# A block with a linear scan and an FP4 feed-forward part: VectorE's order within a slot, later modulation products, a partition maximum through DRAM, and three down products in a row at the end

## The chip, the cores and the metric

The kernel runs on one core of a Trainium2 chip. The time is the device time of one execution in microseconds (us); lower is better. Five engines work side by side, each through its own queue of instructions in order: TensorE (PE; PEld are its weight loads), VectorE (DVE), ScalarE (ACT), GpSimd (POOL) and SyncE (SP), which here only issues DMAs. GpSimd issues some DMAs too. Engines wait for each other through semaphores.

## What is computed

Two batches of 4096 tokens, 512 wide, pass through one block: an adaptive norm, a gated linear recurrence as attention, a second adaptive norm, and a feed-forward part of inner width 1408 whose inputs and weights are rounded to FP4 in blocks of 16 values with one scale each.

```python
mod = (silu(c) @ wmod).reshape(2, 6, 1, -1)
sa, ca, ga, sb, cb, gb = (mod[:, j] for j in range(6))     # ga, gb: |.| floored at 0.25, sign kept
h = layernorm(x) * (1 + ca) + sa
xn = h / norm(h) * sqrt(512) * gamma
q, kv, a = split(xn @ W_qkva.T, 3)
y_t = sigmoid(a_t) * y_{t-1} + kv_t                        # along the tokens
x = x + ga * (q * y)
h = layernorm(x) * (1 + cb) + sb
gate, up = fp4(h) @ fp4(w_gate).T, fp4(h) @ fp4(w_up).T
x = x + gb * (fp4(silu(gate) * up) @ fp4(w_down).T)
```

## The kernel before

Every matrix product runs in three passes over 16-bit halves (high x high, high x low, low x high), so an operand lies in memory as a high and a low part side by side, `hl`, which a transposing DMA on SP turns round.

**The first part** is a loop over slots. There are 16 blocks of 512 tokens (`NBLK`) with 4 feature chunks each (`KC`), so 64 slots with products and 3 more to drain. Slot s issues `mix` s on PE: 36 products of 512 columns, three results (a, kv, q) in three of six PSUM banks, so that mix s + 1 can be in work while mix s is evicted and mix s + 2 cannot. In the same slot the results of mix s - 1 are evicted: `gates` (sigmoid on ACT, L401), `scan` (VectorE, L407, with a small ACT copy `cy` of the last column, L410), `read_out` (VectorE, L416), `halves` (ACT copy L423, transposing DMA of `yt` on SP), and two slots later `joined` (ACT copy L431) and `residual` (GpSimd addition L439 and its DMA to the output, L441). Beside it the slot prepares tokens: `norm_hi` (ACT, L363) and `norm_lo` (VectorE, L368, followed by the transposing DMA of `xT` on SP) for the tile 4 ahead, statistics of the tile 6 ahead (L151, L156, then two small GpSimd steps L158 and L159), `norm_center`, `norm_shift`, `norm_square` and `norm_gain` (L164, L170, L350, L355 and L357) of the tile 5 ahead. The first mix of a block, every fourth slot, needs the block's whole `xT`.

The slots also carry the FP4 weights as units. `plan` gives them to slots: first maxima of blocks (`weight_max`, two units a slot, executed in slots 6 to 22), then `finish_max` (slot 23), which takes the maximum over the partitions with a GpSimd instruction, then one quantizing unit a slot (`quant_rows`, `quant_down`, 34 of them). A unit's weight tile is loaded one slot ahead by SP. `quant` is a chain in seven steps: reciprocal and `sh` (L101, L103); `xn`, `sl`, `she` (L107, L109, L113); absolute value and `sle` on ACT (L116, L118); rounding in two VectorE steps (L120, L123); two products (L125, L127); then a transposing DMA. `Unit.advance(n)` takes one step; the positions of these calls in the loop set where the steps stand in each engine's queue, since the whole order is written out by hand (`manual_schedule`).

The modulation vectors: `mod` 1 and 0 are computed in `start`, 2 in slot 0, and 3, 4 and 5 in slots 1, 2 and 3 (`mod_rows`, L229). `mod_store`, one slot later, copies the two rows by ACT into `row`, whose buffer has the tag of `sig`, and GpSimd sends it to DRAM (`modd`, L259). Each takes 1 MB of weights by `load_mod`. In slots 0 to 2, `hi_qkva` and `lo_qkva` also prepare the weights of the next mix (`wqT`).

**The second part** loops over 64 tiles of 128 tokens. Iteration i issues on PE `products(i)` (72 products, L827) and `down(i - 2)` (33 products, L877), with two PSUM banks for the latter; VectorE, ACT and SP gate, quantize and transpose in between, and `finish` (L897, L900) evicts a down product and adds it to the output by DMA. The last down product is made in two halves of 256 columns.

Of the kernel before, what the change touches and what calls it, by code (L numbers as in the profile page):

```python
# [44 lines left out]
def tile_adaln_block(  # L45
# [51 lines left out]

    def quant(src, sb, rt, nb, hl):

        inv = small.tile([P, nb], F32, name="inv", tag=f"inv{nb}", bufs=2)  # L100
        V.reciprocal(inv, sb)  # L101
        sh = small.tile([P, nb], BF16, name="sh", tag=f"sh{nb}", bufs=2)
        A.activation(sh, sb, AF.Copy, scale=rt)  # L103
        yield
        pool, w = (ring, INTER) if nb == NBH else (work, D)
        xn = pool.tile([P, w], F32, name="xn", tag=f"xn{w}", bufs=1)[:, : nb * QB]
        V.tensor_tensor(blocks(xn), blocks(src), spread(inv, nb), ALU.mult)  # L107
        sl = small.tile([P, nb], F32, name="sl", tag=f"sl{nb}", bufs=2)
        V.scalar_tensor_tensor(  # L109
            out=sl, in0=sb, scalar=rt, in1=sh, op0=ALU.mult, op1=ALU.subtract  # L110
        )
        she = pool.tile([P, w], BF16, name="she", tag=f"she{w}", bufs=1)[:, : nb * QB]
        A.activation(blocks(she), spread(sh, nb), AF.Copy, scale=WPEAK)  # L113
        yield
        a = src
        A.activation(a, xn, AF.Abs, scale=MAGIC)  # L116
        sle = pool.tile([P, w], F16, name="sle", tag=f"sle{w}", bufs=1)[:, : nb * QB]
        A.activation(blocks(sle), spread(sl, nb), AF.Copy, scale=WPEAK)  # L118
        yield
        V.scalar_tensor_tensor(out=xn, in0=a, scalar=FLOOR, in1=xn, op0=ALU.max, op1=ALU.add)  # L120
        yield
        nq = hl[:, 0, :]
        V.scalar_tensor_tensor(out=nq, in0=a, scalar=FLOOR, in1=xn, op0=ALU.max, op1=ALU.subtract)  # L123
        yield
        V.tensor_tensor(hl[:, 1, :], nq, sle, ALU.mult)  # L125
        yield
        V.tensor_tensor(nq, nq, she, ALU.mult)  # L127
# [47 lines left out]
    def load_tile():  # L175
        return work.tile([P, D], F32, name="ld", tag="ld", bufs=7)

# [75 lines left out]
    def mod_store(s, pm):  # L253
        row = apool.tile([B, D], F32, name="row", tag="sig", bufs=1)
        if s == 5:
            signed_floor(row, pm, apool.tile([B, D], F32, name="mag", tag="y", bufs=3))
        else:
            A.activation(row, pm, AF.Copy, bias=1.0 if s in (1, 4) else 0.0)
        G.dma_start(modd[s], row)  # L259
# [203 lines left out]
    def weight_max(wt, am, col, first):  # L463
# [4 lines left out]
        else:  # L468
            m = small.tile([P, 1], F32, name="gm", tag="gm")
            V.tensor_reduce(m, am, AX.X, ALU.max)  # L470
            V.tensor_tensor(gsum[:, col : col + 1], gsum[:, col : col + 1], m, ALU.max)

    def finish_max():
        gs = small.tile([P, 3], F32, name="gs", tag="gs", bufs=1)
        G.partition_all_reduce(gs, gsum, P, bass_isa.ReduceOp.max)
# [12 lines left out]
    def quant_rows(wt, i, am, col):  # L488
        dst = weights(("wgT", "wuT")[col], col, [P, 2 * KC, INTER])
        hl = new_hl()  # L490
        yield from quant(wt, am, rwk[:, col : col + 1], NBX, hl)
        S.dma_start_transpose(dst[:, :, i * P : (i + 1) * P], flat(hl))
# [8 lines left out]
    def quant_down(wt, i, j):  # L501
# [4 lines left out]
        yield from quant(  # L506
            wt, am_d[i][j], rwk[:, 2:3], w // QB, hl.rearrange("p (a d) -> p a d", a=2)
        )
# [10 lines left out]
    for n in range(0, len(downs), 2):  # L519
        plan.append([("maxd", r) for r in downs[n : n + 2]])  # L520
    plan.append([("finish", None)])
    for n, r in enumerate(rows):
# [68 lines left out]
    class Unit:  # L591
# [9 lines left out]
        def advance(self, pos):  # L601
# [4 lines left out]
            elif pos == 3:  # L606
                if self.kind == "max":
                    i, col, _, ams = self.arg
                    weight_max(self.wt, ams[i], col, i == 0)
                elif self.kind == "maxd":  # L610
                    i, j = self.arg
                    weight_max(self.wt, am_d[i][j], 2, self.arg == (0, 0))
                else:
                    finish_max()
# [5 lines left out]
    def start():  # L620
        load_mod(1, 2)
        norm_load(0)
        load_part(0, 2)
        S.dma_start(gam, gamma.partition_broadcast(P))
# [3 lines left out]
        load_part(0, 1)  # L628
        load_mod(0, 2)
        load_part(1, 2)  # L630
# [92 lines left out]
    joining = []  # L723
    NS = NBLK * KC
    plan = [[]] * (KC + 1) + plan
    order = tc.manual_schedule(engines={V.engine, A.engine, G.engine, S.engine, T.engine})
    with order:
        xT = new_xT()
        start()
        for slot in range(NS + 3):  # L730
            i, e = divmod(slot, KC)
            if e == 0 and slot < NS:
                if slot:
                    xT = nxT
                nxT = new_xT() if i + 1 < NBLK else None
            units = [u for u in units + [Unit(*c_) for c_ in coming] if u.step < 7]
            coming = load_units(plan[slot]) if slot < len(plan) else []
            g = slot + KC
# [5 lines left out]
            if slot == 0:  # L744
                cols = mod_columns(2)
            elif slot < KC:
                rows = mod_rows(2 + slot)
            if 0 < slot < 3:
# [3 lines left out]
            if gate is not None:  # L752
                gate = gates(*gate)
            for u in units:
                u.advance(0)
            if len(joining) == 2 or slot >= NS + 2:
# [9 lines left out]
            if slot == 1:  # L766
                signed_floor(gq, cols, atile([P, KC, B], F32, "mag"))
                prep_gain(0)
            if gate is not None:
                joining.append(halves(*read_out(*gate)))  # L770
            if g + 2 < NT:
                norm_moments(g + 2)
                norm_stats(g + 2)
            for u in units:
                u.advance(1)
            if g < NT:
                norm_lo(g, nxT)
            for u in units:
                u.advance(2)
            if g + 1 < NT:  # L780
                norm_center(g + 1)
                norm_shift(g + 1)
                norm_square(g + 1)
                norm_gain(g + 1, G)
            for n in range(3, 7):
                for u in units:
                    u.advance(n)
            if slot < 2:
                scale_qkva(slot + 2)
            if 0 < slot < KC:  # L790
                prep_gain(slot)
            if i == 0 and e < 3:
                load_mod(3 + e)
            if late is not None:
# [14 lines left out]
    tc.no_sync_barrier()  # L809
    assert all(u.step == 7 for u in units)  # L810
    wgT, wuT, wdT = wts["wgT"], wts["wuT"], wts["wdT"]
# [56 lines left out]
    def down(i):  # L868
        hT, u = qh.pop(i)
        width = D // 2 if i == NT - 1 else D  # L870
        pds = []
        for d in range(0, D, width):
            pd = side((P, width))
            n = 0
            for k in range(IC):
                for hp, wp in PASSES:
                    T.matmul(  # L877
                        pd,
                        hT[:, hp * IC + k, :],
                        wdT[:, wd_chunk(wp, k), d : d + width],  # L880
                        start=n == 0,
                        stop=n == 3 * IC - 1,
                    )
                    n += 1
            pds.append(pd)
        return i, pds, u

    def finish(i, pds, u):
        b, t0 = divmod(i * P, N)
# [4 lines left out]
        o = ring.tile([P, D], F32, name="o", tag="o", bufs=3)  # L894
        for n, pd in enumerate(pds):
            d = slice(n * D // len(pds), (n + 1) * D // len(pds))
            V.scalar_tensor_tensor(  # L897
                out=o[:, d], in0=pd, scalar=u, in1=gbs[b][:, d], op0=ALU.mult, op1=ALU.mult
            )
# [10 lines left out]


    with tc.manual_schedule(engines={V.engine, A.engine, G.engine, S.engine, T.engine}):
        h = None
        ended = None
        for i in range(NT + LAG):
            work_i = products(i) if i < NT else None
            ending, ended = ended, down(i - LAG) if i >= LAG else None
            x = None
# [7 lines left out]
            step(h, 2)  # L926
            if work_i is not None:
                sl = silu(0, *work_i)
# [4 lines left out]
            if work_i is not None:  # L933
                gated(0, sl, *work_i)
            step(x)
            if work_i is not None:
                sl = silu(1, *work_i)
            step(x)
            if ending is not None:
                finish(*ending)  # L940
            step(x, 4)
            if work_i is not None:
                gated(1, sl, *work_i)
                gated(2, silu(2, *work_i), *work_i)
                h = quant_h(i, work_i[2])
                step(h, 3)
            else:
                h = None
        finish(*ended)


# [39 lines left out]
```

## Time and profile before

| what | us |
|---|---|
| time, median of 3 runs (1988.0 to 1989.73) | 1988.95 |
| the profiled execution | 1986.11 |
| its span in the profile | 1984.3 |
| PE busy in it | 1920.1 |
| DVE busy | 1622.3 |
| ACT busy | 993.3 |
| POOL busy | 435.2 |
| mean granted PE clock | 0.986 |

A row of the profile's group list shows the source line, the engine and the operation, what is written from what, a count, then busy time and the mean of one in ns, and at the end how long the engine stood idle ahead of it and what ended that. A row of the timeline shows start and length in us and, in brackets, the idle time before it and its releaser. Products on PE are pipelined, and their ends are modelled. A small count of them has no record.

### The profile page before, as it was taken

The numbers are of one execution on the slowest core, as the hardware profiler recorded it, in microseconds if no ns is written. First come the engines' busy times: TensorE is split into PE (matmuls) and PEld (weight loads), VectorE is DVE, ScalarE is ACT, GpSimd is POOL, SyncE is SP. The second block draws the span as 40 slices with busy tenths as digits, with TensorE's granted clock in tenths as the row PEclk, the third lists the DMA queues.
The fourth block names the chain that finished last, engine by engine and source line by source line (L and its number), as shares of the span: only waits on it lengthen the run. The fifth ranks groups of instructions, "written<-read, shape, count | busy, mean of one in ns | idle before, by whom it ended". The sixth has DMA issues, their size and how long they took to land.

```text
span 1984.3 us, 25684 instructions
## 1 busy us (share of the span) xinstructions
PE 1920.1 (97%) x9253; PEld 907.7 (46%) x9253; DVE 1622.3 (82%) x2672; ACT 993.3 (50%) x1704; POOL 435.2 (22%) x602
## 2 busy tenths in 40 slices
PE   7799989999999999999999999999999999999997
PEld 4244434444444444444444444444444444444444
DVE  5679879999966998888888888888888888888874
ACT  3355557777764554444454454455454454444431
POOL 3455546656631110000001001001000000000000
PEclk8999999999999999999999999999999999999998
DMA  7677758888852434334334334434433433433423
GB/s 228 160 180 205 189 143 190 190 185 188 184 134 70 80 69 84 70 62 81 72 61 78 75 62 87 78 62 81 78 62 72 81 62 68 82 64 65 78 46 51
DMA packets 482847, 206.19 MB, mean 104 GB/s; under 512 B 439446, under 2 KB 440726, under 8 KB 482720
## 3 DMA queue, kind: packets, MB, share of 16 engines
q1 hardware_dynamic: 468080, 170.98, 39.6%
q0 software_dynamic: 14640, 33.58, 9.1%
q8 instruction: 72, 1.18, 0.3%
q14 instruction: 55, 0.45, 0.1%
HBM read 62.66 MB, written 33.57 MB: 48 GB/s over the span
## 4 chain that ended last, share of the span: by engine, by line
PE 74%; DVE 12%; issue 8%; ACT 2%; POOL 2%; DMA 2%; SPq 1%; POOLq 0%; DVEq 0%; ACTq 0%
PE mm L827 42%; PE sd L877 21%; PE mm L389 11%; DVE y L407 1%; DVE hl L368 1%; DVE y L416 1%; DVE ld L164 1%; DVE st L151 1%; DVE xn L107 1%; DMA modd<-row 1%; DVE xn L120 1%; DVE ld L170 1%; DVE hl L123 1%; DMA xT<-hl 1%; ACT y L431 0%
## 5 line engine op out<-in xcount | busy, mean ns | idle before, releaser
L827 PEld LDWEIGHTS <-x2T 128*128 128x128 f16 x4608 | 450.9, 98 | 469.8 <-issue 1.5
L389 PE MATMUL mm<-xT,wqT 128*128 128x512 f16 (+1 forms) x2412 | 511.9, 375 | 33.6 <-DMA xT<-hl 23.7
L827 PE MATMUL mm<-wuT,x2T 128*128 128x512 f16 (+1 forms) x2304 | 487.7, 361 | 1.2 <-DVE hid L847 1.2
L827 PE MATMUL mm<-wgT,x2T 128*128 128x512 f16 (+1 forms) x2304 | 487.7, 361 | 0.0
L877 PE MATMUL sd<-wdT,hT 128*128 128x512 f16 (+1 forms) x2145 | 468.9, 377 | 5.0 <-DMA hT<-hhl 5.0
L389 PEld LDWEIGHTS <-wqT 128*128 128x128 f16 x2412 | 232.1, 99 | 315.1 <-issue 46.6
L877 PEld LDWEIGHTS <-hT 128*128 128x128 f16 x2145 | 211.2, 98 | 246.2 <-DMA hT<-hhl 5.5
L842 ACT ACTIVATE silu<-mm,u 128x512 f32<-128x512 f32 (+1 forms) x192 | 124.7, 650 | 293.0 <-PE mm L827 293.0
L847 DVE SCALAR_TENSOR_TENSOR hid<-mm,u,silu 128x512 f32<-128x512 f32 (+1 forms) x192 | 128.5, 672 | 146.1 <-PE mm L827 136.9
L567 POOL TENSOR_SCALAR rstd<-vs 128x1 f32<-128x1 f32 x64 | 14.3, 223 | 987.4 <-ACT sq L565 987.4
L141 ACT ACTIVATE u<-ud,rms 128x1 f32<-128x1 f32 x64 | 18.9, 295 | 278.5 <-DVE rms L137 278.5
L113 ACT ACTIVATE she<-sh 128x512 bf16<-128x512 bf16 (+2 forms) x162 | 149.1, 920 | 4.0
L118 ACT ACTIVATE sle<-sl 128x512 f16<-128x512 f32 (+2 forms) x162 | 146.9, 907 | 0.0
L900 POOL DMA_DIRECT2D out_dram<-o x65 | 57.9, 891 | 283.3 <-DVE o L897 279.5
L120 DVE SCALAR_TENSOR_TENSOR xn<-hid,xn 128x1408 f32<-128x1408 f32 x64 | 103.6, 1618 | 3.7 <-ACT hid L116 3.7
L107 DVE TENSOR_TENSOR xn<-hid,inv 128x1408 f32<-128x1408 f32 x64 | 104.0, 1625 | 2.2
L123 DVE SCALAR_TENSOR_TENSOR hhl<-hid,xn 128x1408 f16<-128x1408 f32 x64 | 104.0, 1625 | 2.2
L145 DVE TENSOR_REDUCE amh<-hid 128x88 f32<-128x1408 f32 x64 | 103.7, 1620 | 2.2
L116 ACT ACTIVATE hid<-xn 128x1408 f32<-128x1408 f32 x64 | 88.2, 1378 | 30.9 <-DVE xn L107 30.9
L423 ACT COPY yh<-y 128x1024 uint16<-128x1024 uint16 x64 | 66.9, 1045 | 70.5 <-DVE y L416 63.8
L439 POOL TENSOR_TENSOR xr<-xr,y 128x512 f32<-128x512 f32 x64 | 81.4, 1271 | 66.4 <-ACT y L431 58.3
L120 DVE SCALAR_TENSOR_TENSOR xn<-ld,xn 128x512 f32<-128x512 f32 (+1 forms) x98 | 66.9, 683 | 28.0 <-ACT ld L116 28.0
(110 smaller groups left out, 1926.6 us busy)
## 6 DMA issues: line engine op xcount, KB each, us to landing
xr<-in_L_attn_x_dram SPq DMA_DIRECT2D x64, 256.0 KB, 3.5
out_dram<-xr POOLq DMA_DIRECT2D x64, 256.0 KB, 4.0
ld<-out_dram SPq DMA_DIRECT2D x64, 256.0 KB, 2.9
out_dram<-o POOLq DMA_DIRECT2D x63, 256.0 KB, 4.0
ld<-in_L_ffn_w_gate_dram SPq DMA_DIRECT2D x22, 256.0 KB, 3.1
ld<-in_L_ffn_w_up_dram SPq DMA_DIRECT2D x22, 256.0 KB, 3.3
scratch<-in_L_wmod_dram SPq DMA_DIRECT2D x4, 1024.0 KB, 5.3
ld<-in_L_ffn_w_down_dram SPq DMA_DIRECT2D x16, 256.0 KB, 3.3
```

Of the source, the lines that this page charges most:

```text
L107: V.tensor_tensor(blocks(xn), blocks(src), spread(inv, nb), ALU.mult)
L113: A.activation(blocks(she), spread(sh, nb), AF.Copy, scale=WPEAK)
L116: A.activation(a, xn, AF.Abs, scale=MAGIC)
L118: A.activation(blocks(sle), spread(sl, nb), AF.Copy, scale=WPEAK)
L120: V.scalar_tensor_tensor(out=xn, in0=a, scalar=FLOOR, in1=xn, op0=ALU.max, op1=ALU.add)
L123: V.scalar_tensor_tensor(out=nq, in0=a, scalar=FLOOR, in1=xn, op0=ALU.max, op1=ALU.subtract)
L145: V.tensor_reduce(am, src.rearrange("p (b k) -> p b k", k=QB), AX.X, ALU.max, apply_absolute_value=True)
L389: T.matmul(pp[:, t : t + width], wqT[:, wp * KC + k, r * P : (r + 1) * P], xT[:, xp * KC + k, t : t + width], start=n == 0, stop=n == 3 * ...
L827: T.matmul(pp[:, : n1 - n0], x2T[:, xp * KC + k, :], wt[:, wp * KC + k, n0:n1], start=n == 0, stop=n == 3 * KC - 1,)
L842: A.activation(sl[:, :w], pairs[j][0][:, :w], AF.Silu, scale=u[:, 0:1])
L847: V.scalar_tensor_tensor(out=hid[:, n0:n1], in0=pairs[j][1][:, : n1 - n0], scalar=u[:, 1:2], in1=sl[:, : n1 - n0], op0=ALU.mult, op1=ALU.mult,
L877: T.matmul(pd, hT[:, hp * IC + k, :], wdT[:, wd_chunk(wp, k), d : d + width], start=n == 0, stop=n == 3 * IC - 1,)
```

## The change

It has six pieces, in the order of the diff.

- `quant` has a switch `late`, used for the weights: the spread of `sh` (`she`) is issued after the absolute value on ACT and not before it.
- `load_tile` has 6 buffers, not 7. `row` has a tag of its own.
- The maximum over partitions: `spread_max` writes the 128 x 3 sums to DRAM and reads them back to every partition (two DMAs on GpSimd's queue) in slot 23. `finish_max`, now in slot 24, reduces them on VectorE. All quantizing units move on by one slot.
- `start` loads the weights of `mod` 0 before the first weights of the products. `mod` 3, 4 and 5 are computed in slots 8, 11 and 14, their weights loaded two slots before.
- The order within a slot: statistics, read-out, lo (and xT's DMA) and then halves; the chain of a unit is spread between the steps of the norm; a unit's first step stands at the end of the slot before it.
- The second part ends differently: iteration 62 issues no down product, iteration 63 issues 60 and 61 after its products, and 62 and 63 follow. The last one is made whole and evicted in two halves.

```diff
-    def quant(src, sb, rt, nb, hl):
+    def quant(src, sb, rt, nb, hl, late=False):
...
-        A.activation(blocks(she), spread(sh, nb), AF.Copy, scale=WPEAK)
+        if not late:
+            A.activation(blocks(she), spread(sh, nb), AF.Copy, scale=WPEAK)
         yield
         a = src
         A.activation(a, xn, AF.Abs, scale=MAGIC)
+        if late:
+            A.activation(blocks(she), spread(sh, nb), AF.Copy, scale=WPEAK)
...
-        return work.tile([P, D], F32, name="ld", tag="ld", bufs=7)
+        return work.tile([P, D], F32, name="ld", tag="ld", bufs=6)
...
-        row = apool.tile([B, D], F32, name="row", tag="sig", bufs=1)
+        row = apool.tile([B, D], F32, name="row", tag="row", bufs=1)
...
+    gmax = dram.tile([P, 3], F32, name="gmax")
+    peaks = []
+    def spread_max():
+        gall = apool.tile([P, P, 3], F32, name="gall", tag="row", bufs=1)
+        G.dma_start(gmax, gsum)
+        G.dma_start(gall, gmax.unsqueeze(0).to_broadcast([P, P, 3]))
+        peaks.append(gall)
     def finish_max():
         gs = small.tile([P, 3], F32, name="gs", tag="gs", bufs=1)
-        G.partition_all_reduce(gs, gsum, P, bass_isa.ReduceOp.max)
+        V.tensor_reduce(gs, peaks.pop().rearrange("p q c -> p c q"), AX.X, ALU.max)
...
+    plan.append([("spread", None)])
     plan.append([("finish", None)])
...
         norm_load(0)
+        load_mod(0, 2)
         load_part(0, 2)
...
-        load_mod(0, 2)
...
+    MODS = {8: 3, 11: 4, 14: 5}
...
-            units = [u for u in units + [Unit(*c_) for c_ in coming] if u.step < 7]
-            coming = load_units(plan[slot]) if slot < len(plan) else []
+            units, coming = coming, load_units(plan[slot]) if slot < len(plan) else []
...
-            elif slot < KC:
-                rows = mod_rows(2 + slot)
+            elif slot in MODS:
+                rows = mod_rows(MODS[slot])
...
-            for u in units:
-                u.advance(0)
...
-            if gate is not None:
-                joining.append(halves(*read_out(*gate)))
             if g + 2 < NT:
                 norm_moments(g + 2)
+            if gate is not None:
+                gate = read_out(*gate)
+            if g < NT:
+                norm_lo(g, nxT)
+            if gate is not None:
+                joining.append(halves(*gate))
+            if g + 2 < NT:
                 norm_stats(g + 2)
             for u in units:
                 u.advance(1)
-            if g < NT:
-                norm_lo(g, nxT)
+            if g + 1 < NT:
+                norm_center(g + 1)
             for u in units:
                 u.advance(2)
+                u.advance(3)
             if g + 1 < NT:
-                norm_center(g + 1)
                 norm_shift(g + 1)
                 norm_square(g + 1)
+            for u in units:
+                u.advance(4)
+            coming = [Unit(*c_) for c_ in coming]
+            for u in coming:
+                u.advance(0)
+            if g + 1 < NT:
                 norm_gain(g + 1, G)
-            for n in range(3, 7):
-                for u in units:
-                    u.advance(n)
+            for u in units:
+                u.advance(5)
+                u.advance(6)
...
-            if i == 0 and e < 3:
-                load_mod(3 + e)
+            if slot + 2 in MODS:
+                load_mod(MODS[slot + 2])
...
-        width = D // 2 if i == NT - 1 else D
...
+        parts = 2 if i == NT - 1 else 1
+        for d0 in range(0, D, D // parts):
...
-        for i in range(NT + LAG):
-            work_i = products(i) if i < NT else None
-            ending, ended = ended, down(i - LAG) if i >= LAG else None
+        for i in range(NT):
+            last = i == NT - 1
+            work_i = products(i)
+            downs = [] if i == NT - 2 else [i - LAG - 1, i - LAG] if last else [i - LAG]
+            ending, ended = ended, [down(d) for d in downs if d >= 0]
...
-        finish(*ended)
+        step(h, 2)
+        finish(*ended.pop(0))
+        step(h, 3)
+        ended.append(down(NT - 2))
+        finish(*ended.pop(0))
+        ended.append(down(NT - 1))
+        for e in ended:
+            finish(*e)
```

More of the change, by code (lines that the diff above doesn't have):

```diff
@@ L4 @@
 import concourse.tile as tile
-from concourse import bass_isa
 from concourse import mybir
@@ L490, in quant_rows @@
         hl = new_hl()
-        yield from quant(wt, am, rwk[:, col : col + 1], NBX, hl)
+        yield from quant(wt, am, rwk[:, col : col + 1], NBX, hl, late=True)
         S.dma_start_transpose(dst[:, :, i * P : (i + 1) * P], flat(hl))
@@ L506, in quant_down @@
         yield from quant(
-            wt, am_d[i][j], rwk[:, 2:3], w // QB, hl.rearrange("p (a d) -> p a d", a=2)
+            wt,
+            am_d[i][j],
+            rwk[:, 2:3],
+            w // QB,
+            hl.rearrange("p (a d) -> p a d", a=2),
+            late=True,
         )
@@ L612, in advance @@
                     weight_max(self.wt, am_d[i][j], 2, self.arg == (0, 0))
+                elif self.kind == "spread":
+                    spread_max()
                 else:
@@ L775, in tile_adaln_block @@
                 u.advance(1)
-            if g < NT:
-                norm_lo(g, nxT)
+            if g + 1 < NT:
+                norm_center(g + 1)
             for u in units:
                 u.advance(2)
+                u.advance(3)
             if g + 1 < NT:
-                norm_center(g + 1)
                 norm_shift(g + 1)
                 norm_square(g + 1)
+            for u in units:
[4 more added lines that the diff above has]
+            if g + 1 < NT:
                 norm_gain(g + 1, G)
-            for n in range(3, 7):
-                for u in units:
-                    u.advance(n)
+            for u in units:
+                u.advance(5)
+                u.advance(6)
+            assert all(u.step == 7 for u in units)
             if slot < 2:
@@ L809, in tile_adaln_block @@
     tc.no_sync_barrier()
-    assert all(u.step == 7 for u in units)
     wgT, wuT, wdT = wts["wgT"], wts["wuT"], wts["wdT"]
@@ L869, in down, with finish @@
         hT, u = qh.pop(i)
-        width = D // 2 if i == NT - 1 else D
[L871 to L888, printed above, removed]
+        pd = side((P, D))
+        n = 0
+        for k in range(IC):
+            for hp, wp in PASSES:
+                T.matmul(
+                    pd,
+                    hT[:, hp * IC + k, :],
+                    wdT[:, wd_chunk(wp, k), :],
+                    start=n == 0,
+                    stop=n == 3 * IC - 1,
+                )
+                n += 1
+        return i, pd, u
+    def finish(i, pd, u):
         b, t0 = divmod(i * P, N)
@@ L894, in finish @@
         o = ring.tile([P, D], F32, name="o", tag="o", bufs=3)
-        for n, pd in enumerate(pds):
-            d = slice(n * D // len(pds), (n + 1) * D // len(pds))
+        parts = 2 if i == NT - 1 else 1
+        for d0 in range(0, D, D // parts):
+            d = slice(d0, d0 + D // parts)
             V.scalar_tensor_tensor(
-                out=o[:, d], in0=pd, scalar=u, in1=gbs[b][:, d], op0=ALU.mult, op1=ALU.mult
+                out=o[:, d], in0=pd[:, d], scalar=u, in1=gbs[b][:, d], op0=ALU.mult, op1=ALU.mult
             )
@@ L913, in tile_adaln_block @@
         h = None
-        ended = None
-        for i in range(NT + LAG):
-            work_i = products(i) if i < NT else None
-            ending, ended = ended, down(i - LAG) if i >= LAG else None
+        ended = []
+        for i in range(NT):
[3 more added lines that the diff above has]
+            ending, ended = ended, [down(d) for d in downs if d >= 0]
             x = None
@@ L926, in tile_adaln_block @@
             step(h, 2)
-            if work_i is not None:
-                sl = silu(0, *work_i)
+            sl = silu(0, *work_i)
             step(x)
@@ L932, in tile_adaln_block @@
             step(x)
-            if work_i is not None:
-                gated(0, sl, *work_i)
+            gated(0, sl, *work_i)
             step(x)
-            if work_i is not None:
-                sl = silu(1, *work_i)
+            sl = silu(1, *work_i)
             step(x)
-            if ending is not None:
-                finish(*ending)
+            for e in ending:
+                finish(*e)
             step(x, 4)
[L942 to L948, printed above, removed]
-        finish(*ended)
+            gated(1, sl, *work_i)
+            gated(2, silu(2, *work_i), *work_i)
+            h = quant_h(i, work_i[2])
+            step(h, 3)
+        step(h, 2)
+        finish(*ended.pop(0))
+        step(h, 3)
+        ended.append(down(NT - 2))
+        finish(*ended.pop(0))
+        ended.append(down(NT - 1))
+        for e in ended:
+            finish(*e)
 _TC = dict(schedule_with_timeline_sim=True)
```

## The prediction

> **What bounds the kernel now.** I read the page's forty slices first, then the groups, then the time stages, then single slots in the timeline.
>
> ```profile
> PE   7799989999999999999999999999999999999997
> DVE  5679879999966998888888888888888888888874
> L389 PE MATMUL mm<-xT,wqT 128*128 128x512 f16 (+1 forms) x2412 | 511.9, 375 | 33.6 <-DMA xT<-hl 23.7
> L877 PE MATMUL sd<-wdT,hT 128*128 128x512 f16 (+1 forms) x2145 | 468.9, 377 | 5.0 <-DMA hT<-hhl 5.0
> ```
>
> TensorE is the bound nearly everywhere; it has holes only in the first 600 us and at the end. The group of the first part's products waits 33.6 us, mostly for the transposed activation tile xT; the down products wait 5.0 us, once. The stages (time, length; busy PE, PEld, DVE, ACT, POOL with counts; clock, DMA share, GB/s):
>
> ```profile
> 135.00:258.00 123.00, 122.86 (x564) 55.49 (x565) 109.37 (x231) 65.32 (x110) 69.88 (x95) 0.99 0.76 195
> 301.00:560.00 259.00, 248.53 (x1130) 110.85 (x1131) 240.25 (x429) 183.99 (x336) 155.84 (x187) 0.99 0.84 186
> 640.00:1870.00 1230.00, 1230.00 (x6044) 591.28 (x6043) 1041.06 (x1630) 589.50 (x990) 100.53 (x173) 1.00 0.39 72
> ```
>
> From 640 to 1870 PE has no hole and the change touches nothing: worth zero. From 135 to 258 PE is full too: the scans (L407) of neighbouring slots come 7.77 us apart, the price of one mix (36 products). From 301 to 560, the slots that quantize weights, VectorE is full (93%) and the scans come 8.35 us apart (7.82 where the weight tile is 384 wide). From mix 4's start (98.08) to mix 63's end (600.99) pass 502.9 us for 60 mixes; 60 x 7.77 is 466.2. So **36.7 us of PE's time are holes or slow clock there**; that, the slow slots before 98, and the tail are all there is to win.
>
> **Part 1, the quantizing slots (34).** Five starts on VectorE in one slot:
>
> ```profile
> 405.51 0.75 DVE L164 SCALAR_TENSOR_TENSOR ld<-xr,mv,mod 128x512 f32<-128x512 f32 x1
> ...
> 406.29 0.75 DVE L170 SCALAR_TENSOR_TENSOR ld<-ld,rstd,mod 128x512 f32<-128x512 f32 x1
> ...
> 406.96 0.68 DVE L120 SCALAR_TENSOR_TENSOR xn<-ld,xn 128x512 f32<-128x512 f32 x1
> ...
> 407.68 0.69 DVE L123 SCALAR_TENSOR_TENSOR hl<-ld,xn 128x512 f16<-128x512 f32 x1
> ...
> 408.48 0.43 DVE L125 TENSOR_TENSOR hl<-hl,sle 128x512 f16<-128x512 f16 x1
> ```
>
> L170 needs L164 and starts 0.03 after its end; L120 does not need L170 and starts 0.08 before its end; L125 needs L123 and starts 0.11 after it. A dependent neighbour costs 0.12 to 0.2 us more. The Trainium skill speaks against this edit: "VectorE: DVE Perf Modes", The DRAIN you can't avoid and Rules for kernel authors, has every operation wait for the pipe to empty, dependent or not, so that only the count matters. The count is the same; by the rule the slot stays at 8.35, by the rows it shrinks. I take the rows.
>
> The new order, start to start: scan 1.10 (1.18 less overlap), bn_stats 0.59, read-out 0.66, lo 0.65, aggregate 0.10, xn 0.58, sl 0.16, center 0.73 (here L120 waits for ScalarE's Abs: the last part's rows put L120 1.47 after xn), L120 0.60, shift 0.66, L123 0.60, next unit's reciprocal 0.26, L125 0.46, L127 0.34: **7.49**. ScalarE adds two short waits of about 0.06: its order is now square, sh, sigmoid (gates the scan), joining copy, hi, cy (gates the read-out). bn_stats fills the old 0.26 wait for cy. Together 7.61, under PE's 7.77 by only 0.16; so PE becomes the bound. 30 slots x 0.58 and 4 x 0.05 give 17.6 of the 36.7; the sum below replaces the whole stretch by 466.2 and adds what stays.
>
> A price not visible before: the residual's GpSimd addition (L439, 1.27) runs beside the scan now; in the new order it reaches over bn_stats and read-out and ends 0.08 before lo (L368) starts. The skill ("SBUF — State Buffer", shared port pair) has a VectorE operation with two SBUF inputs and a GpSimd read exclude each other, a PSUM or single input not. The trace agrees: a lo that met GpSimd's three gamma products (3.72 us from 49.90) took 4.49 instead of 0.75; the scans beside L439 stay at 1.18. So by the rule lo costs nothing if L439 ends first, and up to 1.27 if not: 0 to 1.27 per slot. I take 0.
>
> **Part 2, the maximum.** GpSimd's all-reduce keeps its queue 6.6 us, and with it hi, lo and the next slot:
>
> ```profile
> 264.93 0.38 POOL L475 PARTITION_ALL_REDUCE gs<-gsum  x1 [6.24 <-issue]
> ...
> 301.03 29.33 PE L389 MATMUL mm<-xT,wqT 128*128 128x512 f16 x126 [9.03 <-DMA xT<-hl]
> ```
>
> The scan after it comes 14.4 us after its forerunner, the next two 9.7 and 9.35 apart; PE has lost nothing until mix 28 needs a new xT: 9.03, and some 2.4 to warm up (29.33 for 126 products worth 26.9). New: two DMAs on GpSimd's queue, the second waiting for the first through DRAM. Issue 0.8 and landing 1.6 to 5.2 (the rows of modd, median 2.6), so POOL is held 2.5 to 6 us, with the next tile's L355 and L357 behind it, hence hi and lo; of that some 1.3 reaches lo at the median, 4 at the worst. xT has about 3 us in hand at a block's border (read-out, lo, 3.1 landing against 7.77). finish moves a slot on and adds a 384-element reduction, about 0.6, before rwk, where that slot has no unit. I charge 0.5, bounds 0 to 3.
>
> **Part 3, the modulation products.** The first slots:
>
> ```profile
> 89.27 0.69 ACT L401 ACTIVATE sig<-mm,us 128x512 f32<-128x512 f32 x1 [5.79 <-DMA modd<-row]
> ...
> 77.14 4.88 PE L229 MATMUL sd<-scratch,sc 128*2 128x512 f32 x8 [4.69 <-DMA scratch<-in_L_wmod_dram]
> ...
> 98.08 34.00 PE L389 MATMUL mm<-xT,wqT 128*128 128x512 f16 x144 [4.66 <-DMA xT<-hl]
> ```
>
> row and sig share one buffer, so three sigmoids wait for modd's DMA (13.6 in the group). With its own tag, and the rows gone, slot 3's chain follows slot 2's square at 82.9: sigmoid, scan 83.65, bn_stats, read-out 85.4, lo 86.05, transposing DMA 86.9, landing about 90.0 (98.08 before). mix 3 waits for wqT, not for anything removed: about 78 to 86, so it does not hold mix 4. The two waits of rows 1 and 0 for each other (7.28 on ScalarE, 41 to 48) stay. load_mod(0) earlier puts 1 MB ahead of weights and gamma (some 2.5 us at the 400 GB/s of this stage), while PE's first products are not done before 12.33 anyway and VectorE's chain to mix 0 passes through the weights: -1 to +2, I take +0.5. So mix 4 starts at 90.5, **7.6 earlier**.
>
> The bill: three products of 3.59 (the warm row, 8 instructions at 0.43) move from slots where PE idles into slots 8, 11 and 14, where PE is full: **+10.3**. Their loads (1 MB each) come ahead of xT's transposes in one critical slot (7); 0.5. Stores: 0.6 on ScalarE and at most 1.7 on VectorE, which has 0.8 spare per slot and 3.4 in a slot with such a product: nothing. One ld buffer fewer: two or three are taken per slot, none used longer than two slots: nothing.
>
> **Part 4, order of DMAs.** xT's transpose now goes ahead of yt's on SP. At 559.55 a yt took 2.98 and xT behind it landed at 568; PE waited 3.19. This wait mostly goes, but 7 loads still stand in front: 1.5 left. For other block borders, with DMA at 0.84 x 8.26 / 7.77 = 0.89, another 1.5.
>
> Sum for the first part: 90.5 + 2 (PE cold after its wait for xT) + 466.2 + 10.3 + 4.0 (0.5 + 0.5 + 1.5 + 1.5) = 573.0 against 600.99: **-28.0**.
>
> **Part 5, the tail.**
>
> ```profile
> 1968.70 10.03 PE L877 MATMUL sd<-wdT,hT 128*128 128x256 f16 x66 [4.99 <-DMA hT<-hhl]
> ...
> 1978.78 0.48 DVE L897 SCALAR_TENSOR_TENSOR o<-sd,u,mod_gb 128x256 f32<-128x256 f32 x1 [3.12 <-PE sd L877]
> ```
>
> products(63) now starts at 1927.9 instead of 1935.0, its last gating at 1942.4; 12.6 later (the old chain's 11.9 and one finish) its hT leaves, 7.2 to land: 1962.3. The downs 60, 61, 62 fill PE to 1963.5 (3 x 7.12). The third needs the bank that finish(60) frees at 1953.1, wanted at 1956.4: ready. Down 63 runs warm, 7.12, to 1970.6 instead of 1978.7. Both halves are evicted then, so the second output DMA queues behind the first, +0.85. **-7.4**.
>
> Total -35.4 on a span of 1984.3 (execution 1986.11, which is 2.84 under the runs' median of 1988.95): 1948.9; on the median, **1953.5**.
>
> **Rivals.** (B) Dependent neighbours are not what costs, or L439 meets lo by half: slots at 8.15 to 8.35. For: the skill's rule, a margin of 0.16. Against: the rows above. 11 to 18 more: about 1966 (1964 to 1971). (C) The first slots stay bound by wqT and the DMA queue, mix 4 near 98, while the 10.3 is paid: 1961. For: SP's wqT transposes took 6.5 for three in slot 1. (D) Slower: in every slot lo stands behind the whole residual addition, 1.27. Quantizing slots become 8.9 (8.26 on average before), the maximum's slots 8.2 (VectorE has 6.9 there in the new order): 32 x 0.62 + 17 x 0.4 = 26.6, and the moved products still cost about 7 beside it. The other gains are 7.6 (mix 4), 11.4 (mix 28), 3 (end of the first part) and 7.4 (tail), 29.4: +4, so 1993; it decides from about 1.2 a slot. Against: POOL would have to be late by a whole addition in every slot. (E) The holes close wholly and the products partly hide: 1945.
>
> **Numbers.** Forecast 0.55 (own range 1947 to 1958), B 0.22, C 0.14, D 0.04, E 0.05. Range 1945 to 1968: it takes in C, most of B and all of the forecast. A measurement here tells about 0.2% (4 us) from no change; only D and mishaps of its size lie there: faster 0.95, same 0.01, slower 0.04.
>
> **What would show it.** Scans 7.77 apart between 290 and 540, no PE idle of several us near 300; L368 at 0.75; mix 4 at 90; L229 three times around slots 8 to 14 with 3.5 each; no wait before the last down. Scans at 8.1 or more, or L368 over 1 us, mean B or D; mix 4 after 95 means C.

## The result, and the profile after

| | before | after |
|---|---|---|
| time, median (range of 4 runs each) | 1989.34 (1988.0 to 1989.74) | 1957.37 (1956.05 to 1958.07) |
| ratio, 95% interval | | 0.984 [0.9823, 0.9857] |
| span of the profiled execution | 1984.3 | 1954.2 |
| mix 4 starts on PE | 98.08 | 92.14 |
| first product of the second part on PE | 600.82 | 577.79 |
| from there to the end of the span | 1383.5 | 1376.4 |

The change takes 32 us off; 35.4 were forecast (1953.5, range 1945 to 1968). The page of the changed kernel: the slices, and the two groups of products that waited before.

```profile
PE   6699999999999999999999999999999999999998
DVE  5777879999958988888888888888888888888865
L391 PE MATMUL mm<-xT,wqT 128*128 128x512 f16 (+1 forms) x2412 | 510.2, 375 | 26.9 <-DMA wqT<-hl 13.1
L903 PE MATMUL sd<-wdT,hT 128*128 128x512 f16 x2112 | 465.8, 379 | 0.0
```

The down products wait for nothing any more. The first part's products still wait 26.9, about half of it (7.93 and 5.22) for the weights wqT of slots 2 and 3. The second of these waits, and mix 4:

```profile
79.05 10.77 PE L391 MATMUL mm<-xT,wqT 128*128 128x512 f16 x36 [5.22 <-DMA wqT<-hl]
92.14 39.01 PE L391 MATMUL mm<-xT,wqT 128*128 128x512 f16 x180 [2.32 <-DMA xT<-hl]
```

The stages of the changed kernel (columns as in the prediction): the slots of the maxima, the first quantizing slots, the later ones.

```profile
110.00:258.00 148.00, 148.00 (x660) 63.66 (x659) 116.75 (x257) 71.19 (x122) 69.60 (x106) 1.00 0.76 195
279.00:333.00 54.00, 52.64 (x244) 23.69 (x243) 53.50 (x101) 42.56 (x76) 33.87 (x44) 1.00 0.94 207
340.00:530.00 190.00, 190.00 (x882) 86.09 (x881) 183.36 (x340) 144.78 (x269) 119.80 (x147) 1.00 0.96 199
```

From 279 to 333 VectorE is the bound and catches up: scans 7.56 to 7.57 apart. From 340 to 530 they are 7.77 apart on average and PE has no hole, with DMA at a share of 0.96. What was not foreseen is in the first stage. VectorE is busy for 116.75 of 148, and yet its scans come mostly 8.3 to 8.5 apart (up to 10.2 beside a modulation product), not 7.77. The timeline of one such slot:

```profile
209.60 0.75 DVE L172 SCALAR_TENSOR_TENSOR ld<-ld,rstd,sa 128x512 f32<-128x512 f32 x1
210.44 0.63 ACT L352 ACTIVATE sq<-ld 128x512 bf16<-128x512 f32 x1 [3.32 <-DVE ld L172]
...
211.07 0.67 ACT L403 ACTIVATE sig<-mm,us 128x512 f32<-128x512 f32 x1
...
211.83 1.28 DVE L409 TENSOR_TENSOR_SCAN y<-sig,cy,mm 128x512 f32<-128x512 f32 x1 [1.48 <-POOL ss L357]
```

In the new order a unit of a maximum stands ahead of the shift (L172), and the shift is VectorE's last work in the slot. Square and sigmoid follow on ScalarE, and the next scan needs the sigmoid: VectorE idles 1.48 there in 13 of these 17 slots. The row names POOL as releaser, but the scan does not read ss; sig, which ended at 211.74, is what it reads. PE stays full there all the same because three modulation products of 3.6 fill what the longer slots leave open.

At the end of that stage PE has two holes. GpSimd's two DMAs, what stands behind them, and PE:

```profile
259.10 0.64 POOL L481 DMA_DIRECT2D gmax<-gsum  x1
264.38 0.56 POOL L482 DMA_DIRECT2D gall<-gmax  x1 [4.65 <-DMA gmax<-gsum]
265.93 0.72 ACT L365 ACTIVATE hl<-ld,rn 128x512 f16<-128x512 f32 x1 [4.79 <-POOL rn L359]
...
261.15 32.93 PE L391 MATMUL mm<-xT,wqT 128*128 128x512 f16 x144 [2.55 <-ACT y L433]
295.44 34.92 PE L391 MATMUL mm<-xT,wqT 128*128 128x512 f16 x161 [1.36 <-DMA xT<-hl]
```

GpSimd's queue stands for 5.84 (259.10 to 264.94), and hi waits 4.79 behind it. 144 products are worth 31.08 (4 x 7.77); after the first hole they take 32.93, so 1.85 more go to the slow clock (granted 0.70 from 261.15 to 264 and 0.79 from 264 to 268).

### The profile page after: what moved, and what is told of

Its sections match the earlier page's. It is cut to its first block, busy times and chain, and to the rows that moved or that the text cites. A ratio compares the mean times of both kernels' runs of the same rounds, so it can differ in the third digit from the quotient of the medians.

```text
span 1954.2 us, 25678 instructions
## 1 busy us (share of the span) xinstructions
PE 1909.9 (98%) x9220; PEld 902.4 (46%) x9220; DVE 1607.7 (82%) x2673; ACT 991.3 (51%) x1704; POOL 423.8 (22%) x603
## 3 DMA queue, kind: packets, MB, share of 16 engines
q0 software_dynamic: 14736, 33.78, 10.2%
## 4 chain that ended last, share of the span: by engine, by line
PE 79%; issue 5%; DVE 1%; DMA 1%; ACT 0%; POOL 0%; SPq 0%; POOLq 0%; ACTq 0%; DVEq 0%
PE mm L856 44%; PE sd L903 21%; PE mm L391 14%; DMA ld<-out_dram 0%; POOL out_dram L926 0%; DMA xT<-hl 0%; DVE ld L172 0%; DVE y L418 0%; DVE hl L370 0%; DVE ld L166 0%; DVE st L153 0%; DVE y L409 0%; ACT sq L583 0%; DVE xn L106 0%; SPq L265 0%
## 5 line engine op out<-in xcount | busy, mean ns | idle before, releaser
L391 PE MATMUL mm<-xT,wqT 128*128 128x512 f16 (+1 forms) x2412 | 510.2, 375 | 26.9 <-DMA wqT<-hl 13.1
L903 PE MATMUL sd<-wdT,hT 128*128 128x512 f16 x2112 | 465.8, 379 | 0.0
L903 PEld LDWEIGHTS <-hT 128*128 128x128 f16 x2112 | 206.7, 98 | 242.7
L113 ACT ACTIVATE she<-sh 128x1408 bf16<-128x1408 bf16 (+1 forms) x128 | 128.3, 1003 | 4.0
L409 DVE TENSOR_TENSOR_SCAN y<-sig,cy,mm 128x512 f32<-128x512 f32 x56 | 71.7, 1280 | 49.3 <-ACT sig L403 22.1
L125 DVE SCALAR_TENSOR_TENSOR hhl<-hid,xn 128x1408 f16<-128x1408 f32 x64 | 104.0, 1625 | 2.2
```

The costliest lines, as they stand in the source:

```text
L391: T.matmul(pp[:, t : t + width], wqT[:, wp * KC + k, r * P : (r + 1) * P], xT[:, xp * KC + k, t : t + width], start=n == 0, stop=n == 3 * ...
L903: T.matmul(pd, hT[:, hp * IC + k, :], wdT[:, wd_chunk(wp, k), :], start=n == 0, stop=n == 3 * IC - 1,)
```

## The experiments

Each median is of four runs, with its ratio to runs of the kernel before on the same chip and that ratio's interval. The kernel before took 1989.34 in the result, and 1988.66 beside e1 to e4, 1987.60 beside e5 to e8 and 1987.98 beside e9 to e12. Medians of different sets may thus differ by up to 1.7 for no reason of the edit, and small differences are read from the ratios; the changed kernel has 0.984 [0.9823, 0.9857].

| run | edit to the changed kernel | us | ratio |
|---|---|---|---|
| e1_old_order | old order in the slots | 1976.19 | 0.9936 [0.9919, 0.9952] |
| e2_only_order | kernel before, with the new order alone | 1976.41 | 0.9938 [0.9923, 0.9953] |
| e3_all_reduce | GpSimd's all-reduce | 1963.81 | 0.9877 [0.9862, 0.9891] |
| e4_products_early | modulation products in slots 1 to 3 | 1954.09 | 0.9827 [0.9812, 0.9842] |
| e5_maxima_late | maxima behind the square | 1952.90 | 0.9825 [0.981, 0.984] |
| e6_late_and_early | both | 1943.04 | 0.9778 [0.9763, 0.9792] |
| e7_gpsimd_free | GpSimd's wait split off | 1954.97 | 0.9841 [0.9824, 0.9859] |
| e8_mod0_later | modulation 0's weights at the old place | 1954.61 | 0.9837 [0.982, 0.9853] |
| e9_old_tail | old end | 1961.53 | 0.9868 [0.9846, 0.9889] |
| e10_x1_early | loads of slot 58 spread | 1954.50 | 0.9833 [0.9816, 0.985] |
| e11_joint | e5, e4, e7 and e10 | 1937.98 | 0.975 [0.9734, 0.9766] |
| e12_joint_mod0 | e11 and e8 | 1939.15 | 0.9756 [0.974, 0.9772] |

### The order within a slot

The body of the loop between the gates and the weights' scales was put back, and the spread `she` ahead of the absolute value (e1), or both were taken over alone (e2). The cut shows the start of the body.

```diff
+            for u in units:
+                u.advance(0)
...
+            if gate is not None:
+                joining.append(halves(*read_out(*gate)))
             if g + 2 < NT:
                 norm_moments(g + 2)
-            if gate is not None:
-                gate = read_out(*gate)
-            if g < NT:
-                norm_lo(g, nxT)
...
```

> The changed kernel with the order of the old slots (and she ahead of the absolute value), all else kept. If the start-to-start rows are right (a dependent neighbour costs 0.12 to 0.2 us more), the quantizing slots' scans come 8.35 us apart again and the time rises by 12 to 18, to about 1972. If every VectorE operation waits for the one before it, dependent or not, they stay at 7.77 and the time stays at 1957.

> The kernel before with the new order within a slot alone. The quantizing slots fall to 7.57 to 7.77. The changed kernel's trace shows 8.35 in the slots of the maxima, where VectorE has nothing between the shift and the next scan; if that is the order's doing it comes here too, 16 slots x 0.58 eat 9 of the 18, and the time is about 1980. If the later modulation products caused the 8.35, those slots stay at 7.77 and the time is about 1971.

With the old order the quantizing slots are back at 8.35 and the time rises by 18.8. Only the order was edited, on VectorE, ScalarE and SP, and the number of VectorE's instructions in a slot is the same. So the order makes the difference, not the count. Where it does so, VectorE's rows tell, first in e1 and then in the changed kernel:

```profile
402.75 1.18 DVE L409 TENSOR_TENSOR_SCAN y<-sig,cy,mm 128x512 f32<-128x512 f32 x1
404.19 0.75 DVE L418 SCALAR_TENSOR_TENSOR y<-mm,gq,y 128x512 f32<-128x512 f32 x1 [0.26 <-ACT cy L412]
```

```profile
302.40 1.28 DVE L409 TENSOR_TENSOR_SCAN y<-sig,cy,mm 128x512 f32<-128x512 f32 x1
303.60 0.67 DVE L153 BATCH_NORM_STATS2 st<-xr 128x6 f32<-128x512 f32 x1
304.18 0.73 DVE L418 SCALAR_TENSOR_TENSOR y<-mm,gq,y 128x512 f32<-128x512 f32 x1
...
306.32 0.75 DVE L166 SCALAR_TENSOR_TENSOR ld<-xr,mv,mod 128x512 f32<-128x512 f32 x1
306.99 0.69 DVE L122 SCALAR_TENSOR_TENSOR xn<-ld,xn 128x512 f32<-128x512 f32 x1
307.59 0.75 DVE L172 SCALAR_TENSOR_TENSOR ld<-ld,rstd,mod 128x512 f32<-128x512 f32 x1
308.25 0.69 DVE L125 SCALAR_TENSOR_TENSOR hl<-ld,xn 128x512 f16<-128x512 f32 x1
308.85 0.35 DVE L100 RECIPROCAL inv<-amu 128x32 f32<-128x32 f32 x1
309.11 0.37 DVE L127 TENSOR_TENSOR hl<-hl,sle 128x512 f16<-128x512 f16 x1
```

In the changed kernel each row behind the scan begins 0.08 to 0.09 before the end of the one ahead of it. In e1 the read-out waits 0.26 for ScalarE's copy `cy`, which bn_stats (L153) now covers: 0.34 of the 0.79 between 8.35 and 7.56. The rest is mainly dependent neighbours, as the prediction had read them: e1's slot has five, which start 0.04 to 0.10 after the end of the one ahead, the changed kernel's has one. In e2 the quantizing slots fall to 7.56 and then 7.77, and the maxima's slots, without any modulation product in them, rise from 7.77 to 8.35 to 8.5. The longer slots are thus the order's own doing, and not that of the products. Alone, the order is worth 12 us (1976.41; 1980 had been expected).

### The maximum over the partitions

```diff
-        V.tensor_reduce(gs, peaks.pop().rearrange("p q c -> p c q"), AX.X, ALU.max)
+        G.partition_all_reduce(gs, gsum, P, bass_isa.ReduceOp.max)
...
-    plan.append([("spread", None)])
```

> The changed kernel with GpSimd's all-reduce for the maximum. As predicted (the two DMAs cost 0.5, the all-reduce 11.4) the time rises by about 11, to 1968. If what counts is how long GpSimd's queue is held (5.9 in the changed kernel's trace, 6.6 for the all-reduce), it rises by 0 to 3, to about 1959.

It costs 6.4 (7.4 by the ratios): between the two theories. The timeline of GpSimd in this run shows why the second fell short:

```profile
264.74 0.38 POOL L488 PARTITION_ALL_REDUCE gs<-gsum  x1 [5.85 <-issue]
...
272.01 0.27 POOL L358 TENSOR_SCALAR ss<-ss 128x1 f32<-128x1 f32 x1 [6.88 <-issue]
```

The all-reduce is paid twice. GpSimd stands 5.85 before it, and 6.88 again before its next instruction, waiting for nothing that the profile shows. The kernel before has the same pair, 6.24 and, before its next addition, 7.04. Over 13 us of queue are replaced by 5.84. The first theory fell short as well: PE's hole at that border of blocks is 7.57 here and 1.36 in the changed kernel, but the hole ahead of the second part is 0.99 here and 2.47 there.

### Where the modulation products stand

```diff
-    MODS = {8: 3, 11: 4, 14: 5}
+    MODS = {1: 3, 2: 4, 3: 5}
...
-            if slot + 2 in MODS:
-                load_mod(MODS[slot + 2])
+            if slot + 1 in MODS:
+                load_mod(MODS[slot + 1])
```

> The changed kernel with the products of modulations 3, 4 and 5 back in slots 1, 2 and 3 (the buffer tag of row stays its own). As predicted (PE is full in slots 8 to 14, each product costs 3.5) the time falls by 10 less what the loads disturb, to about 1948 to 1951. If those slots are held at 8.35 by VectorE and ScalarE, most of the products' 10.6 is hidden there, and the time stays within 3 of 1957.

Only 3.3 less (2.6 by the ratios). PE waits for the second theory's reason: without the products it finds holes in the maxima's slots (0.81, 2.74, 0.81 at the blocks' borders of 157, 191 and 225), since the slots there stay at 8.5.

```diff
                 u.advance(2)
-                u.advance(3)
+                if u.kind in ("rows", "down"):
+                    u.advance(3)
...
             for u in units:
+                u.advance(3)
                 u.advance(4)
```

> The changed kernel with the maxima's steps moved from ahead of the norm's shift to behind the square, so that VectorE has work while ScalarE makes square and sigmoid. If that exposed chain (1.5 of idle VectorE a slot) is what makes the maxima's slots 8.35, they fall to 7.77 (longer only with a modulation product) and PE's hole near 261 shrinks: 3 to 6 less, about 1953. If the modulation products or the port make them 8.35, nothing changes: 1957.

> The last run's edit, and the products of modulations 3, 4 and 5 in slots 1, 2 and 3. If the products' 10.6 were hidden only by slots held at 8.35, they show now: 8 to 10 below the last run (10.6 less some 2.5 that the early loads cost in slots 1 to 4), about 1945. If they cost next to nothing wherever they stand, 3 below it, as in the run with them early alone.

With the maxima behind the square the scans come 7.77 apart (11.3 where a product of 3.6 stands), and 4.5 us go (3.0 by the ratios). Now moving the products as well is worth 9.9 within one set of runs, where it had been worth 3.3. Both expectations held: the two edits gain 14.3 together and 7.8 apart (12.3 and 5.6 by the ratios). The profiles agree: the 18 slots from the sixth scan on take 154.8 in the changed kernel, 150.2 in e4, 150.8 in e5 and 139.9 in e6, which is 18 x 7.77. Each alone leaves the other's limit in place, VectorE's 8.35 or PE's 10.6 of extra products.

### GpSimd's wait

```diff
+            if any(u.kind == "spread" for u in units):
+                store_max()
             if gate is not None:
                 gate = gates(*gate)
...
                 norm_gain(g + 1, G)
+            if any(u.kind == "spread" for u in units):
+                spread_max()
```

> The changed kernel, where the write of the sums to DRAM is issued at the start of slot 23 and the read back only behind the gain's two GpSimd steps, so that GpSimd does not stand waiting for the DMA ahead of them. If that wait (4.65, with hi behind it) makes the holes near 261 and 295 (2.55 with 1.85 of slow clock after it, and 1.36), they go: 3 to 5 less, about 1953. If the holes come from VectorE's lag over the maxima's slots, at most 1 less.

2.4 less by the medians, nothing by the ratios (0.9841 against 0.984): the time shows no gain. What the edit moved can only be read from the profiles. PE in this run, and then in e5:

```profile
260.62 79.62 PE L391 MATMUL mm<-xT,wqT 128*128 128x512 f16 x361 [2.41 <-DMA xT<-hl]
```

```profile
290.96 49.38 PE L391 MATMUL mm<-xT,wqT 128*128 128x512 f16 x228 [0.85 <-DMA xT<-hl]
```

The two holes have two causes. Freeing GpSimd removes the second (1.36 at 295; 0.41 to 1.36 in e4, e8, e9 and e10, which leave it alone) and leaves the first. Moving the maxima removes the first and leaves the second, 0.85. So the larger hole came from VectorE's lag over the maxima's slots.

### The first loads

```diff
         norm_load(0)
-        load_mod(0, 2)
...
         load_part(0, 1)
+        load_mod(0, 2)
         load_part(1, 2)
```

> The changed kernel with the weights of modulation 0 loaded at their old place, behind the first weights of the products. The scans of slots 1 and 2 came 1.7 and 1.5 later in the changed kernel than before. If the earlier megabyte did that, this run is 1 to 2 faster, about 1956, with mix 4 near 90.6. If the new order in the slots did it, no change.

2.8 less by the medians, 0.6 by the ratios, with mix 4 at 89.66. But executions scatter here: the scan of slot 1 starts between 64.60 and 66.49 (mean 65.6) in the ten kernels with the early megabyte, and between 64.02 and 64.80 (mean 64.6) in the four without. By these means the early megabyte costs the prologue about 1 us, but the two ranges touch, and in e12 it did not show in the whole.

### The tail and the border of the two parts

The old `down`, `finish` and last loop were put back in e9. In e10 the loads were spread:

```diff
-            if slot == NS - 6:
+            if slot == NS - 8:
                 mods_for(0)
                 gbs[0] = mod_load(5, 0, "mod_gb")
-                x1s = {n: load_x1(n) for n in range(4)}
+            if slot == NS - 7:
+                x1s = {n: load_x1(n) for n in range(2)}
+            if slot == NS - 6:
+                x1s.update({n: load_x1(n) for n in range(2, 4)})
```

> The changed kernel with the old end (down 60 between the last products, the last down in two halves). The prediction's -7.4 for the tail: the time rises by 7 to 8, to about 1964.5, and the wait of 5.0 and the 10.0 for the last down product come back. If the old tail's loss depended on what ran before it, less than 5.

> The changed kernel with the loads of slot 58 spread out: modulation rows in slot 56, the first two tiles of the second part in slot 57, two more in slot 58. If PE's hole of 2.47 near 546 is ScalarE waiting for the first of these tiles with the next sigmoid behind it (4.47 of idle ScalarE), it goes: 2 to 3 less, about 1955. If the transposing DMAs behind the loads make it, the hole stays or moves to another slot: 1957.

The medians differ by 4.2 for the old tail (5.6 by the ratios), less than expected. In the profiles, from the first product of the second part to the end, the three kernels with the old end take 1382.1 (e9), 1382.2 (e2) and 1383.5 (before), and all those with the new one 1376.4 to 1376.9. So 5.2 to 7.1. The wait came back (5.06), but the last down product took 8.85, not 10.03: after that wait the granted clock was 0.50 from 1946.3 to 1949.6 and then 1.00, and in the kernel before 0.50 from 1967.4 to 1974.1.

In e10 the hole near 546 is gone, as its first theory said. The time is 2.9 lower by the medians and 1.4 by the ratios, and the intervals overlap: for one hole of 2.47 the time alone would not decide.

### Together

> Maxima late, products early, GpSimd's wait split off, and the loads of slot 58 spread, all together. Sum of the single readings against the run with late maxima and early products (1943.0): -2.4 for the hole near 534, and 0 to -0.5 for GpSimd, where PE had only 0.37 left to lose: about 1940.5. If the loads moved to slots 56 and 57 delay xT there, 1943.

> The joint version with modulation 0's weights at their old place. If the earlier megabyte costs the prologue 1 to 2, 1 to 2 below the joint run, about 1939. If what the runs of the prologue differ by is scatter, the same as the joint run within 1.

The joint version takes 1937.98, 2.5% under the kernel before, and 5.1 under e6 (5.6 by the ratios), where 2.5 were expected. In e6's profile the hole at 533.62, which e10's edit removes, costs more than its 2.40: the granted clock behind it is 0.50 from 533.95 to 537.3. The stages of the joint version: the maxima's slots and the quantizing ones.

```profile
112.00:240.00 128.00, 128.00 (x595) 58.02 (x593) 113.83 (x246) 69.91 (x118) 75.70 (x100) 1.00 0.78 197
262.00:520.00 258.00, 258.00 (x1198) 116.92 (x1196) 248.72 (x460) 196.78 (x361) 159.20 (x198) 1.00 0.96 203
```

PE is full in both. From mix 4 (92.63, directly behind the last modulation product) to the first product of the second part (558.84) pass 466.2, which is 60 x 7.77: nothing is left to win in this stretch by order. e12 lies 1.2 above it, not below, and the intervals overlap. In its profile PE waited 5.12 for the weights of modulation 4, in e11's 2.05; the two kernels cannot be told apart.

## Why the prediction was right, and where it was off

The forecast's span was 1948.9, the measured one is 1954.2. The 5.3 between them are: mix 4 at 92.14, not 90.5 (1.6); the stretch from there to the second part, 485.65, not 482.5 (3.2); and the rest 1376.4, not 1375.9 (0.5). In the stretch, 60 x 7.77 and three products of 3.53 leave 8.9. The three holes and the slow clock after the first are 8.2 of it, where the forecast had 6.0: 4.0 for holes and 2 for a cold PE behind the wait for mix 4. That last term did not come: the granted clock behind this wait was 1.00 (92.1 to 98).

- **The quantizing slots: right.** 7.49 with two short waits, 7.61 in all, were worked out; VectorE runs at 7.565 where it is the bound, and then PE's 7.77 takes over. That the two agree to 0.05 is in part luck: the scan takes 1.20 to the next start (302.40 to 303.60), not 1.10, and the wait for `cy` does not show. e1 shows that the order did it. The rule of the Trainium skill ("VectorE: DVE Perf Modes", The DRAIN you can't avoid) that every VectorE operation waits for the pipe to empty does not hold for these neighbours: an independent one starts 0.08 before its forerunner's end, here as in the trace before. The prediction took only half of that section, which itself adds that an operation which is not held starts earlier, and refers to Two Vector instructions with no wait between them. Rival B is refuted.
- **GpSimd's addition against lo: right.** L370 has a median of 0.743 from 260 to 540 and takes 0.746 at most. The addition ends 0.33 before it at the median, and never less than 0.11, where 0.08 had been worked out. In this slot read-out begins later:

```profile
403.57 1.27 POOL L441 TENSOR_TENSOR xr<-xr,y 128x512 f32<-128x512 f32 x1 [0.65 <-ACT y L433]
...
405.17 0.74 DVE L370 SCALAR_TENSOR_TENSOR hl<-ld,rn,hl 128x512 f16<-128x512 f32 x1
```

  So the two never met, what a meeting would have cost was not seen, and rival D did not come.
- **The step that failed: the slots of the maxima.** The prediction gave them 6.9 on VectorE "in the new order" and left PE the bound at 7.77. The 6.9 is right as work (8.35 less 1.48), but the wait from shift over square and sigmoid to the scan was counted only for the quantizing slots, where the second rounding (L125 here) and its followers cover it. In the maxima's slots nothing does: 1.48. This made the "+10.3" wrong in kind: the products take PE's time as said (3.53 each), but with longer slots around them taking them out gains 3.3 (e4), and 9.9 only once the slots are short (e6). That the sum still came out is in part luck: over the 18 slots, against e6, the longer slots alone cost 10.4 (e4), the products alone 10.9 (e5), and both together 14.9 and not 21. It also made the larger hole, 2.55 with 1.85 of slow clock, near 261.
- **The maximum: right in direction, the price too small.** 0.5 was charged; the DMA's write to DRAM landed late, near the upper bound given (5.84 of 2.5 to 6), and the hole at 295 it left is 1.36. The prediction counted 6.6 us of GpSimd's queue for the all-reduce and overlooked the 7.04 behind it. The 11.4 ascribed to it were not all its own: putting it back costs 6.4. (They are also 0.3 too many: 126 products at 7.77 for 36 are worth 27.2, not 26.9.)
- **The first slots: right.** Scan 83.65, lo 86.05 and landing 90.0 were about 1 to 2 early for this execution (scan 84.57, mix 4 at 92.14); in the six other runs with the new order and the products in slots 8, 11 and 14 mix 4 stands at 89.66 to 91.96. Mix 3 waited for its weights, as said, but took 10.77 at a granted clock of 0.50 at first (79 to 82) and lasted to 89.8, not to 86: close to holding mix 4 after all. Rival C, mix 4 near 98, is refuted.
- **The border of the parts: a term with the wrong cause.** 1.5 was charged for xT behind loads. The hole is 2.47, and it is ScalarE that waits (4.47) for the first tile of the second part, with the next sigmoid behind it; e10 removes it.

```profile
542.89 0.63 ACT L580 ACTIVATE sq<-ld 128x512 bf16<-128x512 f32 x1 [4.47 <-DMA ld<-out_dram]
...
546.72 31.24 PE L391 MATMUL mm<-xT,wqT 128*128 128x512 f16 x144 [2.47 <-ACT cy L412]
```

- **The tail: right.** -7.4 against -7.1 in the profiles (-5.2 to -7.1 over all of them); the prediction's own terms, 1978.7 to 1970.6 and 0.85 back, give -7.3. The last four down products run without a gap:

```profile
1918.90 28.65 PE L903 MATMUL sd<-wdT,hT 128*128 128x512 f16 x132
```

## What to carry to other kernels

Where one in-order engine is full, look at the start times of neighbours: a chain whose steps follow each other directly costs more than the same steps with a second chain between them. But each step moved away also uncovers what it used to cover, so go through every kind of iteration, not only the one that is to gain: here the change paid back, in the slots of the maxima, what VectorE's last step had hidden. And price moved work against the slot that it lands in as it will be after the change; whether three products cost 3 or 10 depended on which engine held the slot.

## What the runs showed of the hardware that was not expected

- GpSimd's all-reduce keeps its queue twice: 5.85 to 6.24 before it and 6.88 to 7.04 after it in e3, e2 and the kernel before, with 0.38 of shown work.
- A write of 128 x 3 values to DRAM by GpSimd held its successor, which reads it back, until 5.28 after its issue began.
- With the DMA engines at a mean share of 0.96 over 258 us, PE lost nothing to late transposes (e11).
- A hole of about 2.5 in PE's work can bring the slow clock or not: behind the one of 2.55 at 261 the granted clock was 0.70 and 0.79, behind the one of 2.47 at 546.72, in the same execution, it was 1.00 from 546.7 to 554.
